# One of four pair blocks recomputed in the second pass, five of eight differences on GpSimd, and other VectorE forms, in a graph network's first layer

## The chip, the cores and the metric

The kernel runs on one core of one Trainium2 chip. Time is device microseconds for one execution. A kernel is run several times; its time is the median. A profile is taken of one further execution, and the trace of that one is what the views below come from. Engines are named as in the profile: PE (TensorE), ACT (ScalarE), DVE (VectorE), POOL (GpSimd), SP (SyncE, which issues the DMAs here).

## What is computed

Four graph layers over 128 graphs of 128 nodes with 128 features. All but the first are untouched by the change. The first layer, cut to what matters:

```python
h = relu(layernorm(x))                                   # 128 graphs x 128 nodes x 128
D = abs(h[:, :, None, :] - h[:, None, :, :])             # every pair of nodes
z = einsum('bijc,oc->bijo', D, W1) + b1                  # 128 -> 64 channels
m, v = mean(z, axis=(0, 1, 2)), var(z, axis=(0, 1, 2))   # over ALL graphs and pairs
z = leaky((z - m) / sqrt(v + EPS) * g1 + be1)
s = where(adj > 0, einsum('bijo,uo->bij', z, W2) + b2, NEG)
A = softmax(s, axis=-1)
y = (A @ h) @ Wg.T + bg                                  # and a second norm over graphs
```

The mean and variance span all pairs of all graphs, so no pair can be normalised before the last one is made: the layer needs two passes over the pairs. A pair and its mirror have the same value, so the kernel makes each once.

## The kernel before, in words

**Blocks.** A graph's pairs are cut into four blocks (`NQ`). Block `q` holds rows `32 q` to `32 q + 31`, each against the next 64 nodes (blocks 0 and 1) or 63 (blocks 2 and 3), cyclically. So a block is a tile of 128 channels x 2048 (or 2016) differences, and its product with W1 is packed into 128 partitions x 1024 (or 1008) columns: two halves of 64 channels. `first[q]` is the column at which block `q` starts among a graph's 4064 stored columns.

**First pass** (512 blocks in order, graph by graph). `load_norm` loads and normalises four graphs at a time: the statistics, `ln_ve` (L266) and `ln_xn` (L271) on DVE, a power on POOL (L268), a transpose on PE, a ReLU on ACT into the SBUF tile `he`, doubled along its nodes by POOL, and once more into a PSUM tile (`hp`, the tile `pt`). For each block:
- `differences` writes the tile `d`: even blocks on DVE (L378, one input from SBUF, the other from PSUM), odd blocks on POOL (L381, both inputs from `he` in SBUF);
- `products`: Abs in place on ACT (L388), four matmuls on PE (L393) into a PSUM tile `ph`;
- `keep`: ACT copies `ph` to the SBUF tile `v` (L411), DVE takes statistics of it (L413). After the last block DVE aggregates them (L416) and copies the two numbers to `st` (L417). SP writes `v` to HBM after every second block (L420).

Differences are issued three blocks ahead (`AHEAD`) into five `d` buffers; products one block ahead of `keep`.

**Between the passes** the mean and variance become one scale and one bias per channel (`h_sc`, `h_bi`).

**Second pass** (128 graphs in order). `load_pairs` brings a graph's pairs back in two loads (L491), one graph ahead. `graph_scores` applies scale and bias on ACT (L503), the leaky step in place on DVE (L325, `scalar_tensor_tensor` with `v` as both inputs), and the dot with W2 on PE (L511), which adds eight graphs into one PSUM tile. After eight graphs `rows` takes them out on DVE (the us step, L526) and turns them into rows by way of HBM. `attention` then does softmax and the two products for four graphs, a generator whose steps are dealt out, four to a graph, between the scores of later graphs. Its POOL part converts the adjacency and checks it for values other than 0 and 1 (`adf`, `odd`, `sum_odd`, L556 to L560). Its DVE part is negm (L568), u (L569), mx, e, sm, ri, e times ri (L582 to L592), eT, yt, y statistics, and zg (L565).

**Layers 1 to 3** follow, in an order that a planner within the kernel writes out. They share no instruction with the change.

In both passes each engine runs its instructions in the order in which they are queued; the framework adds the waits.

Of the kernel before, what the change touches and what calls it, by code (L numbers as in the profile page):

```python
# [17 lines left out]
P = 128  # L18
EPS = 1e-5
# [3 lines left out]
NQ = P // QR  # L23
GS = 8
# [24 lines left out]
def kernel(ctx: ExitStack, tc: tile.TileContext, x, adj, w, out):  # L49
# [18 lines left out]
    nc.vector.memset(nhalf, -0.5)  # L68

# [181 lines left out]
    NPAIR = QR * (P - 1)  # L251
# [6 lines left out]
    def normalised(pool, xt, G):  # L258
# [11 lines left out]
        for g in range(G):  # L270
            nc.vector.tensor_scalar(  # L271
                xn[:, g, :], xt[:, g, :], mv[:, g, 0:1], rs[:, g : g + 1], ALU.subtract, ALU.mult
            )
# [56 lines left out]
    with tc.tile_pool(name="h_pool", bufs=1) as h_pool:  # L330
# [4 lines left out]
        width = [64 if QR * q < 64 else 63 for q in range(NQ)]  # L335
        first = [QR * sum(width[:q]) // 2 for q in range(NQ)]


        with tc.tile_pool(name="a2", bufs=2) as a2, tc.tile_pool(
            name="a_d", bufs=5  # L340
# [3 lines left out]
            st = a2.tile([P, 2, NB], F32, tag="st", name="st", bufs=1)  # L344
# [18 lines left out]
            def differences(b, q):  # L363


                w_, i0 = width[q], QR * q
# [3 lines left out]
                dv = d[:, 0 : QR * w_].rearrange("p (i j) -> p i j", j=w_)  # L370
                later = hb[:, i0 + 1 : i0 + 1 + w_]
                shifted = bass.AP(
                    tensor=later.tensor, offset=later.offset,
                    ap=[list(later.ap[0]), [1, QR], [1, w_]],
                )
                if q % 2 == 0:
                    own = bcast(hp[:, b % GB, i0 : i0 + QR], 2, w_)
                    nc.vector.tensor_tensor(dv, shifted, own, ALU.subtract)  # L378
                else:
                    own = bcast(hb[:, i0 : i0 + QR], 2, w_)  # L380
                    nc.gpsimd.tensor_tensor(dv, shifted, own, ALU.subtract)  # L381
                return d

            def products(b, q, d):


                n = 8 * width[q]
                nc.scalar.activation(d[:, 0 : 4 * n], d[:, 0 : 4 * n], AF.Abs)  # L388
                ph = a_ph.tile([P, 2, 512], F32, tag="ph", name="ph")
                for t in range(2):  # L390
                    for a in range(2):
                        k = (2 * t + a) * n
                        nc.tensor.matmul(  # L393
                            ph[64 * a : 64 * a + 64, t, 0:n], w1T, d[:, k : k + n],
                            start=True, stop=True,
                        )
                return ph
# [3 lines left out]
            def keep(b, q, ph):  # L401
# [4 lines left out]
                if q % 2 == 0:  # L406
                    kept["v"] = a2.tile([P, 2048], F32, tag="v", name="v", bufs=3)
                v, six = kept["v"], kept["six"]
                at = first[q] - first[q // 2 * 2]
                vq = v[:, at : at + 2 * n].rearrange("p (t e) -> p t e", t=2)  # L410
                nc.scalar.copy(vq, ph[:, :, 0:n])  # L411
# [6 lines left out]
                if q % 2 == 1:  # L418
                    a0 = first[q - 1]
                    nc.sync.dma_start(  # L420
                        pairs_d[b][:, a0 : first[q] + 2 * n], v[:, 0 : at + 2 * n]
                    )

            blocks = [(b, q) for b in range(NB) for q in range(NQ)]
            AHEAD = 3
            load_norm(0)
            ds, phs = {}, {}
            for i in range(-AHEAD, len(blocks)):
# [6 lines left out]
                if 0 <= i + 1 < len(blocks):  # L435
                    phs[i + 1] = products(*blocks[i + 1], ds.pop(i + 1))
# [3 lines left out]
            mean, var = mean_var(a2, [(1.0 / NB, st[:, 0, :], st[:, 1, :])], NB, a_ps)  # L440
# [36 lines left out]
        with tc.tile_pool(name="b2", bufs=2) as b2p, tc.tile_pool(  # L477
            name="b_v", bufs=6
        ) as b_v, tc.tile_pool(name="b_s", bufs=2, space=PSUM) as b_s, tc.tile_pool(
            name="b_ps", bufs=6, space=PSUM  # L480
        ) as b_ps:
            scores = {}
            loads = {}
# [3 lines left out]
            def load_pairs(b):  # L487
                for s in range(2):
                    n = (first + [NPAIR])[2 * s + 2] - first[2 * s]
                    v = b_v.tile([P, 2048], F32, tag="v", name="v")  # L490
                    nc.sync.dma_start(v[:, 0:n], pairs_d[b][:, first[2 * s] : first[2 * s] + n])  # L491
                    loads[b, s] = v, n

            def graph_scores(b):
# [5 lines left out]
                zs = []  # L500
                for s in range(2):
                    v, n = loads.pop((b, s))
                    nc.scalar.activation(v[:, 0:n], v[:, 0:n], AF.Identity, bias=h_bi, scale=h_sc)  # L503
# [699 lines left out]
```

## Time and profile before

| | us |
|---|---|
| median of 3 runs (3989.44 to 4005.87) | 3994.12 |
| the profiled execution | 3991.76 |
| its span, first to last instruction | 3989.6 |
| first pass in it (43 to 1472 us) | 1429 |
| second pass (1472 to 2516 us) | 1044 |
| the other layers (2516 to 3990 us) | 1474 |

Over the whole span PE is busy 74%, DVE 80%, ACT 70% and POOL 34%. HBM is read by 331 MB and written by 297 MB, most of it the stored pairs: 128 graphs x 2032 KB, written once and read once.

How to read the views: a group's line gives source line, engine, operation, output <- inputs, shapes and count, then busy time, mean ns of one, and the engine's idle time before them with what ended it. A chain of waits follows the work that ended last backwards, at each step to what released it. Consecutive instructions of an engine overlap by under 0.2 us in the records, so durations add up to slightly more than the time they take.

### The profile page before, as it was taken

The page shows a single profiled execution, that of the slowest core. Times are in us where ns is not written, and L with a number is a line of the kernel's source. Part 1 is how long each engine was busy: PE and PEld are TensorE (multiplying, and loading weights), DVE is VectorE, ACT ScalarE, POOL GpSimd, SP SyncE. Part 2 cuts the span into 40 slices and gives each one's busy share as a digit, 9 for nine tenths or more (in the row PEclk, how much of TensorE's full clock was granted, in tenths as well). Part 3 has the DMA queues.
Part 4 walks back from the last instruction along what each step waited for, and adds up shares of the span by engine and source line. Part 5 has one row for each costly group of instructions (what it writes and reads, how often), then busy time and mean ns, then how long its engine had stood idle before and what let it go on. Part 6 is the DMA issues. An engine that isn't in the chain of part 4 may idle for free.

```text
span 3989.6 us, 43349 instructions
## 1 busy us (share of the span) xinstructions
PE 2953.6 (74%) x15141; PEld 1455.3 (36%) x15141; DVE 3193.3 (80%) x5106; ACT 2797.5 (70%) x2858; POOL 1357.3 (34%) x746
## 2 busy tenths in 40 slices
PE   5667777777777756666666666688888888888886
PEld 1111111111111111122222222467666666666764
DVE  7999999999999988887878889466666666666663
ACT  5999999999999986555555555265555665666553
POOL 4676667666766641222222213100011100110010
PEclk8999999999999998888888888788898998998987
DMA  3444444444444458877787887200110101101100
GB/s 142 195 199 198 203 200 200 196 203 200 200 197 197 195 213 326 299 281 284 285 295 285 305 291 287 71 25 24 33 38 26 31 27 39 31 26 28 34 10 9
DMA packets 219112, 631.12 MB, mean 158 GB/s; under 512 B 36803, under 2 KB 136453, under 8 KB 186117
## 3 DMA queue, kind: packets, MB, share of 16 engines
q1 hardware_dynamic: 218884, 628.25, 41.6%
q8 instruction: 123, 2.02, 0.2%
q14 instruction: 105, 0.85, 0.1%
HBM read 330.93 MB, written 297.25 MB: 157 GB/s over the span
## 4 chain that ended last, share of the span: by engine, by line
DVE 54%; PE 29%; ACT 7%; DMA 5%; issue 4%; SPq 1%; POOL 0%; ACTq 0%; POOLq 0%; DVEq 0%
DVE six L413 14%; DVE d L378 13%; DVE v L325 10%; PE pa L843 5%; DMA v<-v 3%; PE sc L511 3%; PE po L766 2%; DVE ln_xn L271 2%; ACT d L388 1%; PE pp L852 1%; PE z L727 1%; PE ps L859 1%; PE pv L909 1%; PE pt L719 1%; DMA s<-us 1%
## 5 line engine op out<-in xcount | busy, mean ns | idle before, releaser
L393 PE MATMUL ph<-d,w1T 128*64 128x512 f32 (+1 forms) x4096 | 989.7, 606 | 388.2 <-ACT d L388 315.3
L381 POOL TENSOR_TENSOR d<-he 128x2048 f32<-128x2048 f32 (+1 forms) x256 | 915.6, 3577 | 405.6 <-PE ph L393 399.1
L388 ACT ACTIVATE d<-d 128x2048 f32<-128x2048 f32 (+1 forms) x512 | 1006.2, 1966 | 8.5 <-POOL d L381 5.8
L503 ACT ACTIVATE v<-v,h_bi,h_sc 128x2048 f32<-128x2048 f32 (+1 forms) x256 | 521.7, 2073 | 413.0 <-DMA v<-v 370.0
L511 PE MATMUL sc<-v,w_slide 128*32 128x512 f32 (+1 forms) x2048 | 489.5, 734 | 285.5 <-DVE v L325 285.4
L325 DVE SCALAR_TENSOR_TENSOR v<-v 128x2048 f32<-128x2048 f32 (+1 forms) x256 | 626.9, 2454 | 71.1 <-ACT v L503 70.2
L393 PEld LDWEIGHTS ph<-d,w1T 128*64 128x64 f32 x4096 | 254.8, 137 | 1100.9 <-ACT d L388 789.3
L413 DVE BATCH_NORM_STATS2 six<-ph 128x6 f32<-128x512 f32 (+1 forms) x1024 | 647.7, 675 | 4.8 <-ACT v L411 4.8
L378 DVE TENSOR_TENSOR d<-he,pt 128x2048 f32<-128x2048 f32 (+1 forms) x256 | 575.6, 2249 | 3.7 <-PE ph L393 3.7
L411 ACT COPY v<-ph 128x1024 f32<-128x1024 f32 (+1 forms) x512 | 540.8, 1057 | 14.2 <-PE ph L393 14.1
L704 POOL TENSOR_TENSOR rs<-ve,nhalf 128x4 f32<-128x4 f32 x96 | 112.2, 1169 | 1279.7 <-DVE ve L701 774.2
L731 DVE SCALAR_TENSOR_TENSOR p<-p,q 128x1024 f32<-128x1024 f32 (+1 forms) x192 | 200.1, 1044 | 145.1 <-ACT q L837 54.6
L511 PEld LDWEIGHTS sc<-v,w_slide 128*32 128x32 f32 x2048 | 83.9, 122 | 617.3 <-DVE v L325 480.9
L556 POOL CAST adf<-adj 128x512 f32<-128x512 int32 x32 | 42.8, 1336 | 766.2 <-DMA adj<-in_adj 766.2
L843 PE MATMUL pa<-vals,p 128*128 128x33 f32 x2048 | 270.3, 292 | 23.2 <-DVE p L731 22.9
L843 PEld LDWEIGHTS pa<-vals,p 128*128 128x128 f32 x2048 | 272.4, 213 | 40.4 <-DVE p L731 24.9
L836 ACT ACTIVATE p<-z 128x1024 f32<-128x1024 f32 x128 | 132.6, 1036 | 80.2 <-PE z L727 79.8
L837 ACT ACTIVATE q<-z 128x1024 f32<-128x1024 f32 x128 | 132.9, 1038 | 0.0
L727 PE MATMUL z<-mask,ident_far 128*128 128x512 bf16 x320 | 106.3, 399 | 0.0
L1050 DVE COPY_PREDICATED ps<-mask,ps 128x512 f32<-128x512 int16 x32 | 22.2, 695 | 97.9 <-PE ps L859 88.7
L271 DVE TENSOR_SCALAR ln_xn<-xg,ln_mv,ln_rs 128x128 f32<-128x128 f32 x128 | 97.4, 783 | 3.1 <-POOL ln_rs L268 3.1
L846 DVE RECIPROCAL ri<-pa 128x8 f32<-128x8 f32 x128 | 26.1, 204 | 88.7 <-PE pa L843 88.5
(241 smaller groups left out, 4416.4 us busy)
## 6 DMA issues: line engine op xcount, KB each, us to landing
v<-v SPq DMA_DIRECT2D x256, 1024.0 KB, 5.1
v<-v SPq DMA_DIRECT2D x256, 1008.0 KB, 6.8
xg<-in_x SPq DMA_DIRECT2D x64, 256.0 KB, 3.0
adj<-in_adj SPq DMA_DIRECT2D x64, 256.0 KB, 3.0
u<-s SPq DMA_DIRECT2D x64, 192.0 KB, 4.3
h<-hT SPq DMA_DIRECT2D x32, 256.0 KB, 2.9
y<-yt SPq DMA_DIRECT2D x32, 256.0 KB, 2.1
yt<-y SPq DMA_DIRECT2D x32, 256.0 KB, 2.9
```

The costliest lines, as they stand in the source:

```text
L271: nc.vector.tensor_scalar(xn[:, g, :], xt[:, g, :], mv[:, g, 0:1], rs[:, g : g + 1], ALU.subtract, ALU.mult)
L325: engine.scalar_tensor_tensor(out, v, slope, v, ALU.mult, ALU.max)
L378: nc.vector.tensor_tensor(dv, shifted, own, ALU.subtract)
L381: nc.gpsimd.tensor_tensor(dv, shifted, own, ALU.subtract)
L388: nc.scalar.activation(d[:, 0 : 4 * n], d[:, 0 : 4 * n], AF.Abs)
L393: nc.tensor.matmul(ph[64 * a : 64 * a + 64, t, 0:n], w1T, d[:, k : k + n], start=True, stop=True,)
L411: nc.scalar.copy(vq, ph[:, :, 0:n])
L413: nc.vector.bn_stats(six[:, 2 * q + t, :], ph[:, t, 0:n])
L503: nc.scalar.activation(v[:, 0:n], v[:, 0:n], AF.Identity, bias=h_bi, scale=h_sc)
L511: nc.tensor.matmul(sc[QR * q : QR * q + QR, 0:n], w_slide[:, 30 - 2 * k : 62 - 2 * k], zs[q // 2][:, at : at + n], start=k == 0, stop=k == ...
L731: nc.vector.scalar_tensor_tensor(p, p, FLOOR, q, ALU.max, ALU.max)
L843: nc.tensor.matmul(pa[:, h, :], p[:, h, :], vals[:, i, h, :], start=True, stop=True)
```

## The change

It has three parts, and some buffers move with them.

1. **Block 0 of each graph is no longer stored.** In the first pass it is made for the statistics only: no copy by ACT, and 3040 instead of 4064 columns in HBM (`MADE` = 1024), written in one DMA per graph. In the second pass it is made again: differences on POOL from `hT` in SBUF, two graphs ahead, Abs on ACT and four matmuls on PE one graph ahead, into one PSUM tile (`b_ph`, one buffer); ACT applies scale and bias from there into a tile `z0`. The leaky step runs on `z0` (1024 columns), on block 1 (1024) and on blocks 2 and 3 together (2016): three instructions of each of ACT and DVE instead of two. The pairs are loaded in one DMA, two graphs ahead. `b_ps` goes from six buffers to four.
2. **Five of eight differences of the first pass are POOL's**, three are DVE's (`BY_DVE`); before, four and four. `d` has six buffers, not five, and differences are issued four blocks ahead, not three.
3. **Other VectorE forms.** `ln_ve` is a `tensor_tensor` with a constant tile, `ln_xn` a `scalar_tensor_tensor` whose second tensor is the broadcast `rs`; the aggregation writes `st` itself, without the copy. In `keep`, the statistics are issued before ACT's copy.

```diff
+BY_DVE = 0, 3, 6
...
+    eps = cst("eps", [P, GB])
+    nc.vector.memset(eps, EPS)
...
+    MADE = 16 * width[0]
+    NPAIR = QR * (P - 1) - MADE
...
-        nc.vector.tensor_scalar(ve, mv[:, :, 1], EPS, None, ALU.add)
+        nc.vector.tensor_tensor(ve, mv[:, :, 1], eps, ALU.add)
...
-            nc.vector.tensor_scalar(
-                xn[:, g, :], xt[:, g, :], mv[:, g, 0:1], rs[:, g : g + 1], ALU.subtract, ALU.mult
+            nc.vector.scalar_tensor_tensor(
+                xn[:, g, :], xt[:, g, :], mv[:, g, 0:1], rs[:, g : g + 1].to_broadcast([P, P]),
+                ALU.subtract, ALU.mult,
             )
...
+        def pair_differences(engine, d, hb, own, q):
+            w_, i0 = width[q], QR * q
+            dv = d[:, 0 : QR * w_].rearrange("p (i j) -> p i j", j=w_)
+            later = hb[:, i0 + 1 : i0 + 1 + w_]
+            shifted = bass.AP(
+                tensor=later.tensor, offset=later.offset,
+                ap=[list(later.ap[0]), [1, QR], [1, w_]],
+            )
+            engine.tensor_tensor(dv, shifted, bcast(own[:, i0 : i0 + QR], 2, w_), ALU.subtract)
...
-            name="a_d", bufs=5
+            name="a_d", bufs=6
...
-                if q % 2 == 0:
-                    own = bcast(hp[:, b % GB, i0 : i0 + QR], 2, w_)
-                    nc.vector.tensor_tensor(dv, shifted, own, ALU.subtract)
+                if (NQ * b + q) % 8 in BY_DVE:
+                    pair_differences(nc.vector, d, hb, hp[:, b % GB, :], q)
                 else:
-                    own = bcast(hb[:, i0 : i0 + QR], 2, w_)
-                    nc.gpsimd.tensor_tensor(dv, shifted, own, ALU.subtract)
+                    pair_differences(nc.gpsimd, d, hb, hb, q)
...
-                nc.scalar.copy(vq, ph[:, :, 0:n])
                 for t in range(2):
                     nc.vector.bn_stats(six[:, 2 * q + t, :], ph[:, t, 0:n])
+                if q > 0:
+                    at = first[q] - MADE
+                    vq = v[:, at : at + 2 * n].rearrange("p (t e) -> p t e", t=2)
+                    nc.scalar.copy(vq, ph[:, :, 0:n])
                 if q == NQ - 1:
-                    mv = a2.tile([P, 2], F32, tag="mv", name="mv")
-                    nc.vector.bn_aggr(mv, six.rearrange("p a b -> p (a b)"))
-                    nc.vector.tensor_copy(st[:, :, b], mv)
...
+                    nc.vector.bn_aggr(st[:, b, :], six.rearrange("p a b -> p (a b)"))
+                    nc.sync.dma_start(pairs_d[b], v)
...
-            AHEAD = 3
+            AHEAD = 4
...
             def load_pairs(b):
...
+                v = b_v.tile([P, NPAIR], F32, tag="v", name="v")
+                nc.sync.dma_start(v, pairs_d[b])
+                d = b_d.tile([P, QR * 64], F32, tag="d", name="d")
+                pair_differences(nc.gpsimd, d, hT[:, b, :], hT[:, b, :], 0)
+                loads[b], made[b] = v, d
...
+                v, ph = loads.pop(b), made.pop(b)
+                z0 = b_d.tile([P, MADE], F32, tag="z0", name="z0")
+                z0b = z0.rearrange("p (t e) -> p t e", t=2)
+                nc.scalar.activation(z0b, ph, AF.Identity, bias=h_bi, scale=h_sc)
+                leaky(nc.vector, z0, z0, 0.01)
+                half = first[2] - MADE
+                for part in (v[:, 0:half], v[:, half:NPAIR]):
+                    nc.scalar.activation(part, part, AF.Identity, bias=h_bi, scale=h_sc)
+                    leaky(nc.vector, part, part, 0.01)
...
-            for b in range(NB):
-                if b + 1 < NB:
-                    load_pairs(b + 1)
+            for b in range(-2, NB):
+                if b + 2 < NB:
+                    load_pairs(b + 2)
+                if 0 <= b + 1 < NB:
+                    made[b + 1] = pair_products(b_ph, 0, made[b + 1])
+                if b < 0:
+                    continue
                 graph_scores(b)
```

`pair_products` is the old `products` with its PSUM pool as an argument.

More of the change, by code (lines that the diff above doesn't have):

```diff
@@ L250 @@
     dram = ctx.enter_context(tc.tile_pool(name="dram", bufs=1, space=bass.MemoryType.DRAM))
-    NPAIR = QR * (P - 1)
+    width = [64 if QR * q < 64 else 63 for q in range(NQ)]
+    first = [QR * sum(width[:q]) // 2 for q in range(NQ)]
+    MADE = 16 * width[0]
+    NPAIR = QR * (P - 1) - MADE
     pairs_d = [dram.tile([P, NPAIR], F32, tag=f"v{b}", name=f"v{b}") for b in range(NB)]
@@ L343 @@
         ) as a_ps:
-            st = a2.tile([P, 2, NB], F32, tag="st", name="st", bufs=1)
+            st = a2.tile([P, NB, 2], F32, tag="st", name="st", bufs=1)
             doubled = {}
@@ L477 @@
         with tc.tile_pool(name="b2", bufs=2) as b2p, tc.tile_pool(
-            name="b_v", bufs=6
-        ) as b_v, tc.tile_pool(name="b_s", bufs=2, space=PSUM) as b_s, tc.tile_pool(
-            name="b_ps", bufs=6, space=PSUM
+            name="b_v", bufs=3
+        ) as b_v, tc.tile_pool(name="b_d", bufs=2) as b_d, tc.tile_pool(
+            name="b_s", bufs=2, space=PSUM
+        ) as b_s, tc.tile_pool(name="b_ph", bufs=1, space=PSUM) as b_ph, tc.tile_pool(
+            name="b_ps", bufs=4, space=PSUM
         ) as b_ps:
             scores = {}
-            loads = {}
+            loads, made = {}, {}
             sum_odd = b2p.tile([P, GB, P], F32, tag="sum_odd", name="sum_odd", bufs=1)
@@ L499, in graph_scores @@
                 sc = scores[b // GS]
[L500 to L503, printed above, removed]
-                    leaky(nc.vector, v[:, 0:n], v[:, 0:n], 0.01)
-                    zs.append(v)
+                v, ph = loads.pop(b), made.pop(b)
[7 more added lines that the diff above has]
+                    leaky(nc.vector, part, part, 0.01)
                 for t in range(2):
```

57 lines of the change are left out of this document (17 added, 40 removed).

## The prediction

> **What bounds the kernel now.** I read the busy time by stage first, because the page's shares average three stages with different limits. The columns are the stretch, its length, and busy time and instructions of PE, PEld, DVE, ACT and POOL, then the granted clock, the DMA share and GB/s.
>
> ```profile
> 43.00:1472.00 1429.00, 1007.57 (x4217) 267.53 (x4217) 1414.79 (x1925) 1409.89 (x1085) 966.87 (x346) 0.99 0.48 198
> 1472.00:2516.00 1044.00, 690.48 (x3034) 219.26 (x3034) 849.95 (x768) 538.13 (x287) 238.47 (x130) 0.84 0.78 288
> 2516.00:3990.00 1474.00, 1244.19 (x7853) 962.10 (x7853) 906.11 (x2340) 840.69 (x1474) 139.94 (x257) 0.88 0.10 30
> ```
>
> The first pass has DVE and ACT both busy 99% of its 1429 us: two limits that lie on each other. The second pass is on no engine's limit (DVE 81%) while DMA is at 78%. The layers after 2516 us aren't touched by the change, so their 1474 us stay.
>
> Next, the costly groups on the page, for prices:
>
> ```profile
> L381 POOL TENSOR_TENSOR d<-he 128x2048 f32<-128x2048 f32 (+1 forms) x256 | 915.6, 3577 | 405.6 <-PE ph L393 399.1
> L388 ACT ACTIVATE d<-d 128x2048 f32<-128x2048 f32 (+1 forms) x512 | 1006.2, 1966 | 8.5 <-POOL d L381 5.8
> L503 ACT ACTIVATE v<-v,h_bi,h_sc 128x2048 f32<-128x2048 f32 (+1 forms) x256 | 521.7, 2073 | 413.0 <-DMA v<-v 370.0
> L325 DVE SCALAR_TENSOR_TENSOR v<-v 128x2048 f32<-128x2048 f32 (+1 forms) x256 | 626.9, 2454 | 71.1 <-ACT v L503 70.2
> L411 ACT COPY v<-ph 128x1024 f32<-128x1024 f32 (+1 forms) x512 | 540.8, 1057 | 14.2 <-PE ph L393 14.1
> ```
>
> A difference takes 3.58 us on POOL, its Abs 1.97 us on ACT. ACT idles 370 us behind the loads of stored pairs: this is what fewer stored pairs can win.
>
> Then the timeline at the second pass's end (start, duration, instruction), where POOL and DVE meet:
>
> ```profile
> 2476.72 1.09 POOL L558 TENSOR_TENSOR odd<-adf 128x512 f32<-128x512 f32 x1
> 2476.84 3.09 DVE L325 SCALAR_TENSOR_TENSOR v<-v 128x2016 f32<-128x2016 f32 x1
> ...
> 2477.89 3.17 POOL L559 TENSOR_TENSOR odd<-odd,adf 128x512 f32<-128x512 f32 x1
> ...
> 2481.14 1.27 POOL L560 TENSOR_TENSOR sum_odd<-sum_odd,odd 128x512 f32<-128x512 f32 x1
> 2481.17 3.38 DVE L325 SCALAR_TENSOR_TENSOR v<-v 128x2048 f32<-128x2048 f32 x1
> ```
>
> This carries the prediction. The leaky step (L325, both inputs in SBUF) starts beside L558, which ends at 2477.81, and lasts 2.12 us after that: nearly its whole free 2.23 us. L559 was issued in its middle and ends at 2481.06, 1.13 us after the leaky step's end at 2479.93; free, it takes 1.27 us. The third pair repeats it: 3.38 us, of which 1.24 until POOL's end. So they exclude each other, and only some 0.14 us of each overlap.
>
> Last, the spread of single instructions (min/median/max ns) in the two passes:
>
> ```profile
> L271 DVE TENSOR_SCALAR ln_xn<-xg,ln_mv,ln_rs x116: 269/338/2984, 104.8 to 1289.3; 128x128 f32<-128x128 f32 x116
> ```
> ```profile
> L381 POOL TENSOR_TENSOR d<-he x256: 3548/3579/3603, 35.0 to 1456.1; 128x2048 f32<-128x2048 f32 x128
> L378 DVE TENSOR_TENSOR d<-he,pt x256: 2227/2256/2289, 39.1 to 1455.5; 128x2048 f32<-128x2048 f32 x128
> ```
>
> DVE's own differences, with one input in PSUM, never stretch beside POOL's. The normalisation, SBUF to SBUF, stretches from 0.27 to 2.98 us: it waits for POOL's difference to end, so a difference holds the lock too.
>
> **First pass, per group of four graphs** (44.35 us each between 400 and 1287 us, 32 groups). I take DVE's steps from the chain of waits there, all on DVE, whose shares don't overlap: statistics 42.3% = 18.76 us, differences 39.4% = 17.47, ln_xn 5.5% = 2.44, st copy 3.2% = 1.42, ln_ve 2.6% = 1.15, aggregation 2.7% = 1.20, ln_s and ln_mv 0.94, issue 1.06.
> - DVE makes 6 of 16 differences, not 8: 17.47 x 6/8 = 13.10. The st copy goes. Without waits, ln_xn costs 4 x 0.27 = 1.08 (the new two-input form taken at the price of the old) and ln_ve 0.15. Sum: 13.10 + 18.76 + 1.20 + 0.94 + 1.06 + 1.08 + 0.15 = 36.3 us, plus waits W for POOL.
> - ACT loses 4 copies. In the timeline at 801 us an Abs starts 0.89 us after the copy before it, so 44.35 - 4 x 0.89 = 40.8 us.
> - POOL has 10 differences and 2.0 us of small work: 10 x 3.58 + 2.0 = 37.8 us.
> - So ACT bounds at 40.8 us unless W exceeds 4.5. W is 2.4 now (1.36 for ln_xn, 1.00 for ln_ve), with POOL busy 69% and idle 1.6 us between differences. Afterwards POOL leaves some 0.5 us between two. ln_ve and the first ln_xn meet a running difference and wait half of one on average, 0.88 x 1.8 = 1.6 each; of the next three ln_xn, I let one wait a whole difference, 3.4. W = 6.6, DVE 42.9 us.
>
> Does the new form of ln_xn wait at all? No row has a 128x128 scalar_tensor_tensor with a broadcast input; the nearest is L325, which waits, and I take that. [...] If they didn't wait at all, W would be 0, the first pass ACT's 40.8 us a group, and the total 68 us lower.
>
> First pass: 32 x (42.9 - 44.35) = **-46 us**. Ends: -114 (no waits, ACT bounds) and, with five waits of 2.7 us (the longest seen), 36.3 + 13.5 = 49.8, **+174**. The sixth d buffer and AHEAD = 4 I cost at nothing: POOL's idle, 255 us in 887, is for freed buffers, and that cover is used above.
>
> **Second pass, per eight graphs.** The us step (L526) comes every 64.25 us (963.8 us for 15).
> - Removed: a quarter of the load. DMA moves 289 GB/s x 64.25 us = 18.6 MB; eight blocks less (8 x 0.52 MB) leaves 14.4 MB, 50 us. DMA no longer bounds.
> - DVE: leaky steps of the same 4064 columns, in three instructions. 128 columns cost 0.29 us (L302) and 2048 cost 2.23, so an instruction has a fixed part of some 0.15 us: 8 x (4.46 + 0.15) = 36.9 us. Attention twice: negm 0.43, u 0.42, mx 0.68, e 0.69, sm 0.67, ri 0.18, e*ri 0.69, eT 0.68, yt 0.75, four statistics 0.86, aggregation 0.25, zg 0.67 = 6.97, x2 = 13.9; us 1.48. Sum 52.3, of which 40.0 can't run beside POOL (leaky steps, negm, u, e*ri) and 12.3 can.
> - POOL: 8 new differences of 3.58 - 0.14 = 27.5 us, and twice CAST 0.61, 1.04, 1.27, 1.27, less 0.14 each, = 7.3. Sum 34.8.
> - With POOL's time wholly under the 12.3 us of free DVE work: 40.0 + 34.8 = **74.8 us**. With none of it hidden, and DVE's present idle before u and yt (6.2 us) kept: 52.3 + 34.8 + 6.2 = **93.3 us**. In DVE's order attention steps stand singly between leaky steps, so a POOL difference of 3.4 us covers one step of some 0.65 us in each graph (8 x 0.65 = 5.2), and the 6.2 us of idle: 93.3 - 5.2 - 6.2 = **82 us**.
> - ACT: 8 x (1.97 + 1.06 + 1.06 + 2.07) + 1.3 = 50.6 us, covered. PE: 652 us / 15 = 43.5, plus 8 blocks of 1.93 = 58.9, covered. The products of graph b+1 wait for the read of graph b's single PSUM tile; behind them on PE stand the score products of b, which wait for DVE anyway. Two d tiles keep POOL up to two graphs ahead, so it always has a difference that contests the lock. SP issues one load per graph, not two; POOL's small attention work queues behind up to two differences, 7 us, and only the odd flag needs it.
>
> Second pass: 16 x (82 - 64.25) = **+284 us**, ends +169 and +460.
>
> [...]
>
> **The sum.** The profiled execution took 3991.8 us (span 3989.6), 2.3 below the median of the runs shown. 3991.8 - 46 + 284 = 4229.8, **4230 us**.
>
> **Rivals.**
> - *Good interleaving*: POOL's differences fall under DVE's free work and the normalisation hardly waits: 3991.8 - 114 + 169 = 4047 us. For it: both orders are regular, so phases can lock. Against: one free step at a time stands between leaky steps.
> - *Starved normalisation*: POOL is nearly saturated in the first pass, each of the five short steps waits for a difference, ACT runs dry: 3991.8 + 174 + 284 = 4450 us. For: 2.98 us for a 0.27 us step is there already. Against: while DVE stands, the d buffers fill and POOL pauses.
> - *The lock doesn't bind the new differences* (faster): then the second pass is bounded by PE, DVE with its idle, or DMA at about 60 us: 3991.8 - 46 - 68 = 3878 us. It decides below 64.25 + 46/16 = 67.1 us per eight graphs. For: 34.8 us of POOL is little by itself. Against: the three overlaps above; even perfect hiding gives 74.8.
> - *The change doesn't do what it says*: ln_xn and ln_ve keep sharing, which is in the forecast; if they don't, W = 0 gives 3991.8 - 114 + 284 = 4162 us.
>
> **How the numbers follow.** Forecast (with the last rival's small shift) 60%, good interleaving 15%, starved normalisation 17%, no binding lock 6%, a half-binding lock near no change 2%. The range leaves out the faster cases and the far end of starvation: 4070 to 4420. This kernel's runs can't tell less than about 0.5% from no change. Faster 0.06, same 0.02, slower 0.92.
>
> **What would show it.** Right: leaky steps and POOL's second-pass differences both stretch (differences of 5 us and more); ACT idles behind DVE, not DMA; DVE near 100% busy for some 1310 us; the us step every 82 us; the first pass ends some 46 us earlier with ln_xn above 1 us. Wrong: second-pass differences at 3.6 us with leaky steps at 2.2 us, or a us step under 67 us.

## The result, and the profile after

The changed kernel takes 4411.78 us, median of 4 runs (4402.63 to 4422.68). The kernel before, run beside it, takes 3997.73 us (4 runs). The ratio is 1.104, 95% interval 1.100 to 1.107: **10% slower**. The profiled execution took 4402.63 us (span 4400.8), to be set against the 3991.76 us of before.

First, busy time by stage, cut as in the prediction: first pass, second pass, other layers. Columns: stretch, length, busy time and instructions of PE, PEld (PE's weight loads), DVE, ACT, POOL, granted clock, DMA share, GB/s.

```profile
43.00:1479.00 1436.00, 1044.21 (x4217) 277.86 (x4217) 1291.96 (x1735) 1306.83 (x957) 1193.67 (x411) 0.95 0.36 149
1479.00:2925.00 1446.00, 1057.56 (x4058) 311.00 (x4058) 1212.65 (x894) 804.67 (x543) 793.39 (x258) 0.85 0.47 162
2925.00:4401.00 1476.00, 1245.24 (x7853) 965.88 (x7853) 907.58 (x2341) 841.59 (x1474) 139.10 (x257) 0.88 0.10 30
```

The 411 us lie in the second pass, 1446 us against 1044. The first pass, which lost a quarter of its copies, is no shorter (1436 against 1429), and now **no** engine is full in it: DVE 90%, ACT 91%, POOL 83%. The other layers stand still.

To compare kernels I use three marks in each trace: the last write of `st` ends the first pass; the first layer-1 product ends the second; the us step gives the second pass per eight graphs. Before: 1472.3 us, then 1069.5, then 1447.7 of other layers. After: 1478.9, 1472.2, 1449.8. So the first pass gave +6.6, the second +402.7, the rest +2.1. The other layers are the same code in all kernels here and took 1442 to 1469 us from run to run; a single total therefore carries some 15 us of scatter, and the stages are the better measure: the second pass of four kernels that have the same code there (after, even_odd, forms, recompute_only) lies between 1471.6 and 1472.5 us, and the first pass of four others that share it (after, no_read, b_d4, no_read_d4) ends between 1478.6 and 1486.4.

The costly groups on the page of after. `L353` is `pair_differences`, `L359` the Abs, `L334` the leaky step, `L512` scale and bias on the stored blocks; after the bar stand busy time and mean ns, then idle time before the group and what ended most of it.

```profile
L359 ACT ACTIVATE d<-d 128x2048 f32<-128x2048 f32 (+1 forms) x640 | 1201.9, 1909 | 256.5 <-POOL d L353 251.3
...
L353 POOL TENSOR_TENSOR d<-hT 128x2048 f32<-128x2048 f32 x128 | 538.9, 4220 | 602.8 <-PE ph L364 602.8
...
L334 DVE SCALAR_TENSOR_TENSOR v<-v 128x1024 f32<-128x1024 f32 (+1 forms) x256 | 619.0, 2434 | 11.3 <-ACT v L512 11.3
...
L512 ACT ACTIVATE v<-v,h_bi,h_sc 128x1024 f32<-128x1024 f32 (+1 forms) x256 | 408.5, 1643 | 63.3 <-DMA v<-v 54.6
...
L334 DVE SCALAR_TENSOR_TENSOR z<-z 128x1024 f32<-128x1024 f32 x128 | 333.0, 2602 | 85.0 <-ACT z L508 84.5
```

What the change was able to win, it won: ACT's wait for loads fell from 370.0 us to 54.6. Against that, two things. The leaky step on `z`, 1024 columns, takes 2602 ns in the mean, more than 2048 columns do when free (2.23 us). And POOL, which makes the new differences in 4220 ns each, stood idle for 602.8 us before them, waiting for products on PE.

The spread of the same instructions (min/median/max ns):

```profile
L334 DVE SCALAR_TENSOR_TENSOR v<-v x256: 1155/2251/5650, 1510.0 to 2904.6; 128x1024 f32<-128x1024 f32 x128
...
L334 DVE SCALAR_TENSOR_TENSOR z<-z x128: 1159/2294/4309, 1494.0 to 2900.2; 128x1024 f32<-128x1024 f32 x128
```
```profile
L353 POOL TENSOR_TENSOR d<-hT x128: 3595/4037/5617, 1477.3 to 2861.7; 128x2048 f32<-128x2048 f32 x128
```

Both sides stretch: the `z` step from 1.16 us up to 4.3, the difference from 3.6 up to 5.6. The timeline shows how (start, duration, instruction, idle time before it):

```profile
2004.46 4.33 POOL L353 TENSOR_TENSOR d<-hT 128x2048 f32<-128x2048 f32 x1 [25.66 <-PE ph L364]
...
2005.85 4.02 DVE L334 SCALAR_TENSOR_TENSOR v<-v 128x1024 f32<-128x1024 f32 x1
...
2009.29 4.03 POOL L353 TENSOR_TENSOR d<-hT 128x2048 f32<-128x2048 f32 x1 [0.51 <-PE ph L364]
2010.39 4.02 DVE L334 SCALAR_TENSOR_TENSOR z<-z 128x1024 f32<-128x1024 f32 x1
```

POOL's first difference ends at 2008.79; the leaky step issued in its middle ends at 2009.87, 1.08 us later, nearly its whole free time. The second pair repeats it: POOL ends at 2013.32, the leaky step at 2014.41. That is the lock of the prediction. But before the first pair POOL had stood for 25.66 us, waiting for PE, while DVE ran leaky steps of 1.2 and 2.25 us undisturbed. The waits between 1579 and 2910 us, fifteen us steps (engine, line, releaser, us in total, times, longest):

```profile
POOL d L353 <- PE ph L364: 552.1, 74, 25.8
...
ACT d L359 <- POOL d L353: 219.1, 78, 10.2
...
ACT z L508 <- PE ph L364: 126.6, 44, 6.8
...
DVE mx L590 <- PE pl L585: 87.3, 30, 5.2
...
DVE z L334 <- ACT z L508: 63.1, 30, 6.8
```

Read them as a ring: POOL waits for PE to finish with a `d` buffer, ACT's Abs waits for POOL, the `z` read on ACT waits for PE's products, DVE's leaky step waits for ACT; and PE's score products wait for the leaky step (PEld 240.9 us, PE 151.9 us, same view). On PE the products of the next block 0 stand between those score products, so the ring closes. DVE, never idle by the forecast, was idle for 185 of these 1331 us. That these waits close into one chain is read from the views and the kernel's order; the experiments say what it is worth.

### The profile page after: what moved, and what is told of

Read it like the earlier page. It is cut to its first block, busy times and chain, and to the rows that moved or that the text cites. A ratio compares the mean times of both kernels' runs of the same rounds, so it can differ in the third digit from the quotient of the medians.

```text
span 4400.8 us, 45202 instructions
## 1 busy us (share of the span) xinstructions
PE 3358.2 (76%) x16165; PEld 1560.9 (35%) x16165; DVE 3435.0 (78%) x5043; ACT 2962.0 (67%) x2986; POOL 2138.9 (49%) x938
## 4 chain that ended last, share of the span: by engine, by line
PE 31%; DVE 24%; issue 6%; ACT 4%; POOL 1%; DMA 0%; SPq 0%; DVEq 0%; ACTq 0%; POOLq 0%
DVE v L334 8%; PE pa L854 5%; PE sc L519 4%; DVE z L334 3%; PE ph L364 3%; PE po L777 2%; DVE u L577 1%; PE pp L863 1%; PE ps L870 1%; PE pv L920 1%; PE z L738 1%; PE pl L582 1%; PE pt L730 1%; PE pl L584 1%; PE pd L1032 1%
## 5 line engine op out<-in xcount | busy, mean ns | idle before, releaser
L364 PE MATMUL ph<-d,w1T 128*64 128x512 f32 (+1 forms) x5120 | 1386.6, 641 | 413.1 <-ACT d L359 371.2
L359 ACT ACTIVATE d<-d 128x2048 f32<-128x2048 f32 (+1 forms) x640 | 1201.9, 1909 | 256.5 <-POOL d L353 251.3
L353 POOL TENSOR_TENSOR d<-he 128x2048 f32<-128x2048 f32 (+1 forms) x320 | 1142.1, 3586 | 227.1 <-PE ph L364 145.3
L353 POOL TENSOR_TENSOR d<-hT 128x2048 f32<-128x2048 f32 x128 | 538.9, 4220 | 602.8 <-PE ph L364 602.8
L334 DVE SCALAR_TENSOR_TENSOR v<-v 128x1024 f32<-128x1024 f32 (+1 forms) x256 | 619.0, 2434 | 11.3 <-ACT v L512 11.3
L519 PE MATMUL sc<-v,w_slide 128*32 128x504 f32 (+1 forms) x1536 | 441.7, 676 | 171.0 <-DVE v L334 169.4
L421 ACT COPY v<-ph 128x1008 f32<-128x1008 f32 (+1 forms) x384 | 386.3, 1008 | 123.8 <-issue 69.2
L512 ACT ACTIVATE v<-v,h_bi,h_sc 128x1024 f32<-128x1024 f32 (+1 forms) x256 | 408.5, 1643 | 63.3 <-DMA v<-v 54.6
L353 DVE TENSOR_TENSOR d<-he,pt 128x2016 f32<-128x2016 f32 (+1 forms) x192 | 431.2, 2246 | 0.0
L334 DVE SCALAR_TENSOR_TENSOR z<-z 128x1024 f32<-128x1024 f32 x128 | 333.0, 2602 | 85.0 <-ACT z L508 84.5
L519 PE MATMUL sc<-z,w_slide 128*32 128x512 f32 x512 | 295.9, 663 | 96.1 <-DVE z L334 96.1
L508 ACT ACTIVATE z<-ph,h_bi,h_sc 128x1024 f32<-128x1024 f32 x128 | 153.3, 1198 | 240.9 <-PE ph L364 140.9
```

Of the source, the lines that this page charges most:

```text
L334: engine.scalar_tensor_tensor(out, v, slope, v, ALU.mult, ALU.max)
L353: engine.tensor_tensor(dv, shifted, bcast(own[:, i0 : i0 + QR], 2, w_), ALU.subtract)
L364: nc.tensor.matmul(ph[64 * a : 64 * a + 64, t, 0:n], w1T, d[:, k : k + n], start=True, stop=True,)
L508: nc.scalar.activation(z0b, ph, AF.Identity, bias=h_bi, scale=h_sc)
L512: nc.scalar.activation(part, part, AF.Identity, bias=h_bi, scale=h_sc)
L519: nc.tensor.matmul(sc[QR * q : QR * q + QR, 0:n], w_slide[:, 30 - 2 * k : 62 - 2 * k], z[:, t * n : t * n + n], start=k == 0, stop=k == 2 ...
```

## The experiments

Two theories for the second pass. **Lock** (L in the expectations): its loss is DVE and POOL excluding each other in SBUF (in the trace of before some 0.14 us of such a pair overlapped). **Ring** (R): its loss is the new chain POOL, ACT, PE, ACT, DVE, PE through few buffers, whatever POOL does in it. For the first pass: the split (five of eight on POOL) eats what the missing copies gave, or the new forms do, or the buffers. Each kernel ran once, but for every_4th (ten runs) and every_2nd (four).

All second-pass figures are us per eight graphs, the mean of fifteen us steps; "busy" is DVE's between the first and last of them, and counts waiting for the lock as busy, since the instruction is under way. Overlaps of the records are counted once.

| kernel | us step | DVE busy | DVE idle |
|---|---|---|---|
| before | 64.3 | 53.5 | 10.8 |
| after | 88.6 | 76.3 | 12.3 |
| no_read | 72.9 | 52.6 | 20.3 |
| b_d4 | 83.8 | 74.8 | 9.0 |
| no_read_d4 | 69.1 | 53.4 | 15.7 |
| paced_diff2 | 79.0 | 71.7 | 7.3 |

### no_read: the ring without POOL's reads

```diff
-                pair_differences(nc.gpsimd, d, hT[:, b, :], hT[:, b, :], 0)
+                nc.gpsimd.memset(d, 0.5)
+                nc.gpsimd.memset(d[:, 0:1536], 0.5)
```

> The changed kernel, but in the second pass GpSimd fills the tile d with a constant by two memsets (2048 and 1536 columns, about 3.6 us by the 0.52 us of the 512-column memset in the trace of before) in place of the 3.58 us difference. Left out: the differences of block 0 in the second pass, so its pairs are constant there. The chain of buffers and waits is the same; GpSimd only no longer reads SBUF there. Theory L (VectorE's two-input steps and GpSimd's differences exclude each other, and that sets the second pass): the us step falls from 88.7 us per eight graphs to 62-70 (PE, busy 66 us, is the next limit), leaky steps return to 1.2 and 2.2 us; total about 4400 - 16 x 22 = 4050 us. Rival R (the ring difference -> Abs -> products -> one PSUM tile -> z0, with the products queued behind score products on PE, sets it, and the exclusion matters little): the us step stays at 84-89 us, total 4340-4410.

Measured: 4148.69 us, the second pass 1212.4 us instead of 1472.2. The leaky steps of this kernel (min/median/max ns):

```profile
L334 DVE SCALAR_TENSOR_TENSOR v<-v x256: 1158/2187/3317, 1504.1 to 2644.2; 128x1024 f32<-128x1024 f32 x128
...
L334 DVE SCALAR_TENSOR_TENSOR z<-z x128: 1160/1225/2304, 1492.1 to 2639.8; 128x1024 f32<-128x1024 f32 x128
```

Beside memsets, which only write, the `z` step has a median of 1225 ns instead of 2294, and DVE is busy for 52.6 us, where the prediction's sum without waits was 52.3. So the stretch is the lock: without it DVE's time falls by 23.7 us. But only 15.7 of these reach the end, because DVE's idle time grows by 8.0: the ring's part. What is left over before, 72.9 - 64.3 = 8.7 us, holds no lock that before does not have too. The us step lies between the two theories (62 to 70 and 84 to 89 us): neither held alone. The two memsets take 1.80 and 1.38 us, 0.40 less than a difference, so up to 8 x 0.40 = 3.2 of the 15.7 could be a shorter ring: the lock is worth 12.5 to 15.7.

### paced_diff2: the lock without the ring

The kernel before, with a block-0 difference per graph on POOL of which only one column is read, by an ACT instruction that also waits for that graph's first leaky step; no Abs, no products.

```diff
                     loads[b, s] = v, n
...
+                d = b2p.tile([P, QR * 64], F32, tag="d", name="d")
+                nc.gpsimd.tensor_tensor(
+                    d.rearrange("p (i j) -> p i j", j=64), shifted, bcast(hb[:, 0:QR], 2, 64),
+                    ALU.subtract,
+                )
+                extra[b] = d
...
                     zs.append(v)
...
+                nc.scalar.activation(
+                    seen, extra.pop(b)[:, 0:1], AF.Identity, bias=zs[0][:, 0:1], scale=1.0
+                )
```

> paced_diff again, now with the pace held: ScalarE reads one column of the difference's tile with a bias column of that graph's pairs after the leaky step, so the read can't be moved ahead of its graph (in paced_diff it was, and the differences ran back to back). One difference per graph over the whole second pass; no product or score hangs on it. Theory L (exclusion alone, without the changed kernel's ring): by VectorE's 51 us and GpSimd's 35 us per eight graphs, of which 5 to 12 us can overlap, the us step is 74-84 us, total 4150-4310. Rival (the exclusion costs only what no_read gave back, 15.7 us, because the second pass has DMA waits to hide it in): 66-73 us, total 4020-4130.

Measured: 4244.63 us, second pass 1313.5, us step 79.0. Its leaky steps, and its second-pass differences:

```profile
L325 DVE SCALAR_TENSOR_TENSOR v<-v x256: 2220/3086/5684, 1481.6 to 2738.6; 128x2048 f32<-128x2048 f32 x128
```
```profile
L500 POOL TENSOR_TENSOR d<-hT x128: 3594/4047/5896, 1491.2 to 2722.3; 128x2048 f32<-128x2048 f32 x128
```

One difference a graph that nothing needs costs 14.7 us per eight graphs, 1.84 us each, and stretches both sides as in the changed kernel. The ACT read is a new wait too, but not one that reaches DVE: between the first and last us step the leaky steps wait for ACT's `v` for 35.1 us, against 59.3 in the kernel before. DVE's busy time grows by 18.2 us, of which 3.5 are taken from its idle time. The cost lies within the 12.5 to 15.7 of the run before: adding the lock and taking it away give about the same size, though the two kernels have different loads beside it. Over 16 steps it is 200 to 250 us of the second pass's 403. **Both theories hold**, the lock for the larger part.

### beside_diff and paced_diff: two attempts at the same that failed

In beside_diff the difference is issued with nothing that reads it; in paced_diff ACT reads it ahead of the scale and bias, where it is one copy of `d[:, 0:1]`.

```diff
+                nc.scalar.copy(seen, extra.pop(b)[:, 0:1])
                 zs = []
```

> The kernel before, with one more instruction per graph: a GpSimd difference of block 0 into a tile that nobody reads, issued with the loads of the second pass. No chain hangs on it. Theory L: it costs nearly what it costs in the changed kernel, since VectorE's 51 us and GpSimd's 35 us per eight graphs can overlap by 5 to 12 us only: the us step goes from 64.25 to 74-84 us, total 4150-4310. Rival R: GpSimd has the time (24% busy), nothing waits for it: 64-66 us, total 3990-4020.

> The kernel before with one GpSimd difference per graph into a tile of which ScalarE reads one column in that graph's turn, so that the differences come one per graph over the whole second pass and not back to back as in beside_diff. No product or score hangs on them. Theory L (exclusion of two-input VectorE steps): 51 us of VectorE and 35 us of GpSimd per eight graphs can overlap little; the us step is 74-84 us, total 4150-4310. Rival (what cost 389 us in beside_diff was only the starvation of negm behind back-to-back GpSimd instructions): 65-69 us, total 4000-4070.

Measured: 4385.15 and 4370.17 us. In neither did the differences come one a graph. POOL ran them back to back: in beside_diff the us steps are 112.4, 131.1 and 292.8 us apart and then 63 to 65, in paced_diff 177.5, 177.5, 137.5 and then 62 to 66. ACT's early read made ACT wait for POOL (277 us between 1540 and 1900), not POOL for the graph. As prices of one difference among other work they say nothing: of beside_diff's 389 us, 162 are a single `negm` that was under way while POOL ran 42 differences (last section).

### b_d4 and no_read_d4: four difference buffers

```diff
-                d = b_d.tile([P, QR * 64], F32, tag="d", name="d")
+                d = b_d.tile([P, QR * 64], F32, tag="d", name="d", bufs=4)
```

b_d4 has this edit in the changed kernel, no_read_d4 has it with the memsets of no_read.

> The changed kernel with four d buffers in the second pass in place of two, so that GpSimd's next difference no longer waits for the products of the graph before last (552 us of idle in 1331 us in the changed kernel's trace). Theory L: the two engines exclude each other whenever the differences come; the us step stays at 84-89 us, with GpSimd's idle now behind other waits, total 4340-4410. Rival R: the ring opens, the us step falls to 74-80 us, total 4180-4260.

> no_read and b_d4 in one: memsets for the differences of the second pass (left out: those differences, a constant stands for them), and four d buffers. If the 8.7 us per eight graphs that no_read still stands above the kernel before come from the ring of buffers (GpSimd idle behind the products), the us step falls from 72.9 to 65-69 us, total 4020-4090. If they come from the order of work on PE, which has 8 more products and is busy 61 us, it stays at 71-73 us, total 4120-4150.

Measured: 4359.65 us, us step 83.8 (second pass 62 us shorter); and 4102.48, us step 69.1 (61 shorter than no_read). Each fell between what its two theories said, the first near the lock's, the second near the buffers'. So two more buffers loosen the ring by 4 to 5 us per eight graphs, with the lock or without. Of its 8.7 us some 4.8 remain (69.1 - 64.3), and no run says to what they belong: the single PSUM buffer, the place of the products in PE's order, the third leaky step, or the pools that the change also altered (`b_ps` from six buffers to four, and `b_v`, which the description of the change leaves out, from six tiles of half a graph to three of a whole one).

### beside_memset: POOL busy, no reads, no ring

The memsets of no_read, added to the kernel before with nothing that reads them.

> The kernel before, with two GpSimd memsets per graph (2048 and 1536 columns, about 3.6 us) into a tile that nobody reads, where the kernel beside_diff has the difference. Theory L, if it is GpSimd's reads of SBUF that exclude VectorE's two-input steps: no cost, 64-66 us per eight graphs, total 3990-4020. If any GpSimd access excludes them: like beside_diff, 74-84 us. Rival R: 64-66 us.

Measured: 4072.28 us, second pass 1150.6, 81 us over before, though the leaky steps beside memsets last 2.23 to 2.25 us, their free time. The loss sits in three us steps, of 97.5, 105.1 and 73.4 us; the others take 60 to 67. In each of the three DVE stood in one instruction, `negm`, for 36.4, 40.8 and 11.7 us (0.41 when free): 88 us together over its free time, about what was lost. Outside these three, the us steps show no price of POOL work that doesn't read (60 to 67 us, against 62 to 65 in the kernel before). The last section comes back to it.

### even_odd, forms, recompute_only: the first pass taken apart

even_odd goes back to four of eight differences on POOL and keeps all else; forms goes back to the old `ln_ve` and `ln_xn` and keeps the split; recompute_only does both, so that the recomputing and its buffers are left.

```diff
-BY_DVE = 0, 3, 6
+BY_DVE = 0, 2, 4, 6
```
```diff
-        nc.vector.tensor_tensor(ve, mv[:, :, 1], eps, ALU.add)
+        nc.vector.tensor_scalar(ve, mv[:, :, 1], EPS, None, ALU.add)
...
-            nc.vector.scalar_tensor_tensor(
-                xn[:, g, :], xt[:, g, :], mv[:, g, 0:1], rs[:, g : g + 1].to_broadcast([P, P]),
-                ALU.subtract, ALU.mult,
-            )
+            nc.vector.tensor_scalar(
+                xn[:, g, :], xt[:, g, :], mv[:, g, 0:1], rs[:, g : g + 1], ALU.subtract, ALU.mult
+            )
```

> The changed kernel with GpSimd and VectorE taking four of eight differences each, as before; all else is kept. Theory (five of eight leaves GpSimd so full that the first pass waits on its rhythm): a group of four graphs takes VectorE 36.3 + 4.4 + waits of 2.4 = 43.1 us, ScalarE 40.8, against 45.2 us now; the first pass ends about 60 us earlier, at 1410-1440 us. Rival (the split hardly matters, or the waits fill what it frees): 1465-1495 us.

> The changed kernel with the old forms of ln_ve and ln_xn (tensor_scalar); all else is kept, the aggregation into st too. Theory W (the new forms read two SBUF tensors and wait for GpSimd's differences as the old ones did): the first pass ends within 12 us of the changed kernel's 1479 us. Rival (the new forms share less): it ends 30 to 100 us later. Third (an old form is passed over between back-to-back GpSimd instructions, as negm was in beside_memset): single ln waits of more than one difference, over 4 us, and an end 30 to 150 us later.

> The changed kernel with both the old split (four differences of eight each) and the old forms of ln_ve and ln_xn: the recomputed block alone, with the aggregation into st and the buffers. Theory (in even_odd the ln waits vanished because of where the steps fall between differences, not because of the form): 40.4 us per group of four graphs as in even_odd, first pass ending at 1340-1365 us, total 4270-4300. Rival (with GpSimd less full the new forms do share less): ln waits of 2 to 3 us per group return, 42-44 us per group, first pass ending at 1400-1450 us, total 4330-4390.

| kernel | split | forms | end of first pass | us per four graphs | total |
|---|---|---|---|---|---|
| before | 4 of 8 | old | 1472.3 | 44.3 | 3991.8 |
| after | 5 of 8 | new | 1478.9 | 45.2 | 4402.6 |
| forms | 5 of 8 | old | 1465.9 | 44.4 | 4409.7 |
| even_odd | 4 of 8 | new | 1349.1 | 40.4 | 4285.2 |
| recompute_only | 4 of 8 | old | 1349.4 | 40.4 | 4277.6 |

The split alone costs 130 us with the new forms and 117 with the old ones. Without it the recomputing, with the aggregation into `st` and the buffers, takes 123 us off the first pass, and the second pass stays where it was (1472.3 us in recompute_only). The forms are worth nothing: with the even split the old ones end 0.3 us later, with the other split 13 us earlier, little more than such ends scatter. The middle of the first pass in even_odd (busy time, 400 to 1287 us), and its normalisation:

```profile
400.00:1287.00 887.00, 671.82 (x2904) 225.24 (x2900) 870.74 (x1251) 887.00 (x659) 664.80 (x242) 1.00 0.41 168
```
```profile
L274 DVE TENSOR_TENSOR ln_ve<-ln_mv,eps x32: 135/148/163, 29.6 to 1293.7; 128x4 f32<-128x4 f32 x32
```

ACT is busy for all of the 887 us, and `ln_ve` never waits. That isn't the form, since in recompute_only the old one has 141 to 171 ns: it is where the step falls. In even_odd none of the 110 `ln_ve` and `ln_xn` steps of this stretch starts inside a difference of POOL's, in the kernel before 59 of 99 do. I had let one meet a difference, and expected 43.1 us per four graphs. The even split doesn't ensure this place: in every_2nd (below), with the same split and the old forms, `ln_ve` has a mean of 824 ns. In the changed kernel the same stretch reads

```profile
400.00:1287.00 887.00, 641.98 (x2586) 168.96 (x2586) 805.08 (x1078) 804.82 (x588) 737.05 (x254) 0.95 0.36 150
```

and DVE's groups in it (busy time, mean ns, idle time before):

```profile
L417 DVE BATCH_NORM_STATS2 six<-ph 128x6 f32<-128x512 f32 (+1 forms) x630 | 397.5, 676 | 80.6 <-PE ph L364 80.3
...
L279 DVE SCALAR_TENSOR_TENSOR ln_xn<-xg,ln_mv,ln_rs 128x128 f32<-128x128 f32 x80 | 76.8, 1018 | 0.0
L274 DVE TENSOR_TENSOR ln_ve<-ln_mv,eps 128x4 f32<-128x4 f32 x19 | 52.1, 2742 | 0.0
```

The five short steps wait here (`ln_ve` 2742 ns for 0.15 us), and DVE is idle for another 80.6 us behind the products. Nobody is full, so the three engines wait for each other: `ln_ve` and `ln_xn` hold up DVE's differences, then ACT and PE run dry, then POOL waits for buffers (94.5 us for PE and 37.3 us for ACT in this stretch). That the split does it is shown; the chain in this sentence is my reading of the waits. Whether it is the number of POOL's differences or their order (with five of eight POOL makes two blocks in a row) no run separates.

### every_4th and every_2nd: fewer graphs recomputed

The kernel before, with block 0 recomputed in every fourth (every second) graph only, the difference issued on POOL two graphs ahead, the product one; old forms and even split, with six `d` buffers, `AHEAD` 4, the aggregation into `st` and four `b_ps` buffers. The edit is that of every_4th; every_2nd has `b % 2 == 1`.

```diff
+        def again(b):
+            return b % 4 == 1
...
-                nc.scalar.copy(vq, ph[:, :, 0:n])
+                if q > 0 or not again(b):
+                    nc.scalar.copy(vq, ph[:, :, 0:n])
...
+                if b + 2 < NB and again(b + 2):
+                    pair_differences(nc.gpsimd, d, hT[:, b + 2, :], hT[:, b + 2, :], 0)
```

> A version in between: the differences alternate between VectorE and GpSimd as before, the aggregation writes st itself, six d buffers; block 0 is made again for one graph in four only, straight into its place in v; the others are stored whole. First pass: ScalarE saves one copy of 0.89 us per group of four graphs, 44.35 - 0.9 = 43.4 us, some 25-30 us earlier than before. Second pass per eight graphs: DMA 60.5 us instead of 64.25; GpSimd's exclusive time 7.3 + 2 x 3.44 = 14.2 us, VectorE 51 us, together under 64 if a third is hidden: 60-66 us. Total 3920-4000. If two differences per eight graphs cost what they cost in the changed kernel (24.4 / 8 = 3 us each): 66-70 us, total 4000-4060.

> The same with one graph in two. First pass: 44.35 - 1.8 = 42.6 us per group, some 55-60 us earlier than before. Second pass per eight graphs: DMA 57 us; GpSimd's exclusive time 7.3 + 4 x 3.44 = 21.1 us and VectorE 51, of which at most 12 hidden: 61-72 us. Total 3890-4060. If each difference costs 3 us as in the changed kernel: 70-76 us, total 4030-4130.

| differences added | first pass | second pass | per difference | ratio to before |
|---|---|---|---|---|
| 32 (every_4th) | -10 us | +34 us | 1.06 us | 1.003 (1.000 to 1.005) |
| 64 (every_2nd) | -25 us | +131 us | 2.05 us | 1.022 (1.019 to 1.025) |
| 128 (recompute_only) | -123 us | +403 us | 3.15 us | one run, 285 us over |

The price per difference is net of the load that it saves. Every fourth graph costs 0.3%, with an interval that barely leaves out no change; every second costs 2%. The us steps, 65.7 and 71.7, lie where the two sides of each expectation meet. Both first passes gained less than expected (25 to 30 and 55 to 60 us). Once they run evenly, after some 7 and 14 of the 32 groups, they take 43.7 and 42.8 us per four graphs, near the 43.4 and 42.6 that were expected; what is missing was lost in the groups before, of up to 51 and 52 us, and why stays open. No version beats the kernel before: the second pass takes back more than the first one gives, in each of the three.

## Why the prediction was right, and where it was not

The sign, the place and the cause came out: slower by the lock in the second pass, with other layers unchanged. The size did not. It said +238 us, the profiled execution shows +411, and the range (to 4420) just held the median, by 8 us; of the four runs one, 4422.68, lies above it. That is in part luck: the range reached so far up for a starved first pass, and what used it up was mostly the second pass. The missing 173 us are 53 in the first pass, 119 in the second and 2 behind it.

- **DMA no longer bounds, ACT and PE are not full**: right. DMA's share of the second pass fell from 0.78 to 0.47. ACT is busy 49.8 us per eight graphs (50.6 said), PE 66.0 of 88.6 (58.9 said). DVE's work without the new waits is 52.6 in no_read (52.3 said). This is closer than it should be: the forecast's sum counts the records' overlaps twice, and no_read's time holds some waits for POOL's attention steps.
- **A difference on POOL holds up the leaky step**: right. The forecast let DVE wait 29.6 us per eight graphs (82 less 52.3) and never idle; it waits 24.0 (76.3 less 52.3) and is idle for 12.3. The lock was overcounted by a fifth, and the idle time was put at nothing. The forecast's split of DVE's steps agrees with the trace of after where the two engines met there: `u` took 3.82 us in each of the 14 cases (of 32) in which it started inside a difference (0.41 when free), and e times ri 1.52 us in the 14 (of 30) inside an `odd` step (0.68 free), while e from `pl`, sm, the y statistics and the us step started inside a POOL instruction 13, 13, 52 and 27 times and stayed within 0.02 us of their shortest. No `negm` met one in after; in before 9 of 32 did and took 1.26 us.
- **"Two d tiles keep POOL up to two graphs ahead, so it always has a difference that contests the lock"**: wrong, and with it "score products behind them wait for DVE anyway". POOL stood 552 us for PE. I added up each engine's work and called PE covered by its busy time; but its *order* puts block 0's products among score products that wait for DVE, and so ties five engine steps into a ring. Without the lock that ring still costs 8.7 us per eight graphs, 139 us in all, and four `d` buffers give back about half. This is the step that failed in the second pass.
- **First pass, -46**: wrong by 53 us. W, DVE's wait for POOL, was near: 4 x (1.02 - 0.27) + (2.74 - 0.15) = 5.6 us per four graphs (6.6 said). What failed is taking DVE's sum for the time: beside its waits DVE is idle 4 us per four graphs (80.6 us in 887), for products, and I had "the cover is used above" for POOL's idle time without asking what three engines near their limit do to each other. ACT's bound of 40.8 us was right, and the sixth buffer and `AHEAD` 4 do cost nothing: even_odd has both and reaches that bound with 40.4.
- **A slip in the sum**: 16 x (93.3 - 64.25) is 465, not the 460 given as the second pass's far end; nothing else uses it.
- **The signs named ahead**: both kinds of instruction did stretch (differences to 5.6 us, with a median of 4.0), and ln_xn is at 1.02 us. Four did not come: ACT waits most for POOL (219 us of 1331) and PE (127), not for DVE (66); DVE is busy 86%, not near 100%; the us step is 88.6, not 82; the first pass ends 7 us later, not 46 earlier.
- **New forms**: "ln_xn and ln_ve keep sharing" was right (1018 and 2742 ns in the mean, at least 331 and 133 each); they also gain nothing where nothing shares (even_odd ends its first pass at 1349.1 us, recompute_only at 1349.4).
- **Rivals**: the total lies nearest *starved normalisation* (4450), but not by its mechanism: the first pass lost 7 us, not 174. *Good interleaving* did come about in the first pass, once the split was undone.

## What to carry to other kernels

Before moving work to GpSimd beside VectorE, read from a trace which of VectorE's steps stretch beside GpSimd's, and what share of its time they are. Here the leaky step, with both inputs in SBUF, went from 1.16 us to a median of 2.29 us on `z`, while VectorE's differences, with one input in PSUM, stayed at 2.23 to 2.28 us, though 108 of 192 started inside one of GpSimd's. Each 3.6 us difference cost 1.06 us when rare, 1.84 when paced one to a graph, and 3 when every graph also waited for it (the first and the last net of the loads saved). A sum of busy times is a lower bound; where a new block runs through four engines and back, write down in which queue each of its steps stands and what is ahead of it there, and give the first link buffers for the longest wait. In the first pass two engines were both at 99%; giving one of them's work to a third, beside which its short steps stretched (`ln_ve` to 2742 ns for 0.15 us), left all three waiting (91%, 91% and 83% busy between 400 and 1287 us): try such a split by itself.

## What the runs showed of the hardware that I had not expected

A `negm` of 0.41 us was under way for 36.39 us in beside_memset and for 161.75 us in beside_diff, far longer than any one POOL instruction beside it (at most 1.80 and 3.60 us). In beside_memset (timeline: start, duration, instruction), DVE first:

```profile
1697.79 2.23 DVE L325 SCALAR_TENSOR_TENSOR v<-v 128x2048 f32<-128x2048 f32 x1
1699.93 36.39 DVE L571 TENSOR_SCALAR negm<-adj 128x512 f32<-128x512 int32 x1
1736.24 2.65 DVE L325 SCALAR_TENSOR_TENSOR v<-v 128x2016 f32<-128x2016 f32 x1
```

and POOL:

```profile
1697.87 2.69 POOL L495 MEMSET d<- 128x1536 f32 x2
1700.51 3.55 POOL L494 MEMSET d<- 128x2048 f32 x2
...
1731.17 3.55 POOL L494 MEMSET d<- 128x2048 f32 x2
1734.66 1.38 POOL L495 MEMSET d<- 128x1536 f32 x1
```

`negm`, a `tensor_scalar` with one input that takes 0.41 us when free, stood for 36 us while 23 memsets began and ended back to back, and finished 0.28 us after the last of them. The longest in that kernel is 40.8 us; in beside_diff one took 161.7 us, through 42 differences and 11 of POOL's attention steps, and ended 0.28 us after the difference behind which POOL stood idle. In beside_memset POOL did not pause: the wait above ended beside a CAST of POOL's (`adf`, 0.79 us from 1735.99); but in beside_diff two such CASTs (0.61 us each, at 1950.83 and 2054.43) ran while `negm` stood. The leaky step, with two inputs, was not held up by the same memsets (2.23 us above), and beside differences the longest that I found is 5.69 us (beside_diff), 3.5 over its free time, less than one difference of 3.6. `negm` doesn't always stand so long: at 1607 us of beside_diff, where POOL and DVE had been taking turns, it took 3.82 us, 3.4 over its free time. In the two long cases shown here (36.39 and 161.75 us) POOL's instructions had kept their free times, back to back, for at least 6.9 and 7.1 us before it came. Whether that is the condition no run settles. In the changed kernel `negm` wasn't touched by it (411 to 427 ns); there none of the 32 started inside an instruction of POOL's.
